# Attention on TensorE: written order, mixing in one piece, score banks spaced evenly

## The chip, the cores and the metric

The kernel runs on one core of a Trainium2 chip. The metric is the device time of one execution in microseconds (us). The core has five engines with an instruction stream each: TensorE (PE, with its weight loads as PEld), VectorE (DVE), ScalarE (ACT), GpSimd (POOL) and SyncE (SP), which here issues most of the DMAs. An engine works through its own stream in order and waits at semaphores for the others. All data is 32-bit floating point.

## The reference

The input x has 8 sequences of 512 tokens with 256 features. Four layers follow each other, each applied to the layer norm of x and added to x: a scan layer, a mixture of experts, causal attention, and the same mixture of experts again (same weights). Cut to what matters here:

```python
def _L0_attn_b_ref(x, Wqkv, Wout):
    B, T, D, H = (1, 1024, 256, 16)
    DK = D // H
    SCALE = 1.0 / float(np.sqrt(DK))
    ...
    scores = jnp.einsum('bhtd,bhsd->bhts', q, k) * SCALE
    scores = jnp.clip(scores, -10.0, 10.0)
    mask = jnp.triu(jnp.full((t, t), NEG, dtype=scores.dtype), k=1)
    scores = scores + mask[None, None, :, :]
    attn = jax.nn.softmax(scores, axis=-1)
    out = jnp.einsum('bhts,bhsd->bhtd', attn, v)
    out = out.transpose(0, 2, 1, 3).reshape(b, t, d)
    return jnp.einsum('btd,ed->bte', out, Wout)
...
x = x + _L0_attn_a_ref(_layernorm(x, axis=-1), ...)
x = x + _L0_ffn_ref(_layernorm(x, axis=-1), ...)
x = x + _L0_attn_b_ref(_layernorm(x, axis=-1), L0_attn_b_Wqkv, L0_attn_b_Wout)
x = x + _L0_ffn_ref(_layernorm(x, axis=-1), ...)
return x
```

Attention has 16 heads of 16 features, and t is 512. The mixture of experts has two shared experts, which see every token, and 16 routed ones, of which each token takes four, chosen by a router.

## The kernel before, in words

The kernel has four stages. A scan stretch runs the scan layer over the eight sequences and, in between, the shared experts and the routing of the sequences that are through. A routed stage then works off the routed experts of all tokens in blocks of 128 rows. An attention stretch does the same for attention and the second mixture, and a second routed stage ends the kernel. The change touches the attention stretch, about 810 to 1374 us of the profile.

**Attention of one sequence** (`main` of class `Attention`, line 998). Keys lie with the features of a head on 32 partitions, so that four heads stand in the four quarters of the array's rows. The 16 heads make four groups of four, (o, w). The weights of a group are made in three score steps (`weights`, line 1003): step 0 holds the first block of 128 keys against 512 queries, step 1 the fourth and the second block (128 and 384 queries), step 2 the third (256). What lies above the causal diagonal isn't computed. A step's matmuls (L1020, tile `ps_a`) use a quarter of the rows each and run side by side; they fill two PSUM tiles of kind `pair`, two banks each, of which there are two in all. ScalarE takes the exponentials (L1031, two per step, into `es_a` or a free part of `w_all`), and VectorE clips and masks (L1034, L1042).

**Mixing** (`mix`, line 1047) multiplies the weights with the values. Its matmuls (L1055, tile `po_a`) write 32 columns of the array each, again four side by side, and add up over the key blocks in one PSUM bank of kind `one`, of which there are four. A column of ones among the values gives the softmax's sum. `share` (line 1065) copies the sums on ScalarE (L1068), turns them with four TensorE transposes (L1071, tile `pto_a`) and divides on VectorE (L1073, L1074). After the four groups the output is turned (`turned`, line 353) and projected (`add_projection`, line 408).

**Order around the change.** Work is written as Python generators that yield a number of columns, their estimated TensorE work. `beside` (line 310) draws the next step from the piece that is least advanced by its share, and `timed` (line 326) places steps at given fractions of the whole. Beside attention of sequence b run: the projection to q, k, v of sequence b+1 (tiles `pq_a`, `pv_a`), the shared experts of sequence b-2 (`pg_m`, `pd_m`), routing of b-1 (transposes `pt_m`, router scores `pl_m`, counts `pr_m`), the norm and transposes of b+2 (`pt_l`) and scatters on POOL. Sequences 0 and 1 have no shared experts beside them, and sequence 7 has no projection. In the steps of attention, a score step of a group alternates with a mixing step of the group before:

```python
for i in range(len(BANKS)):
    yield weights(o, w, i, at)
    if last is not None:
        yield mix(*last[0:2], i, last[2])
if last is not None:
    share(*last)
```

This written order is where the scheduler of the tile framework starts, which then orders each engine's stream by when it takes the inputs to be ready. So in the compiled program neighbouring instructions of a step can be pulled apart. Buffers and semaphores follow from its order.

Of the kernel before, what the change touches and what calls it, by code (L numbers as in the profile page):

```python
# [15 lines left out]
P = 128  # L16
# [54 lines left out]
def tile_hybrid_block(  # L71
# [224 lines left out]

    class Piece:
# [48 lines left out]
    def issue(piece):  # L348
        for _ in piece.steps:
            pass  # L350


    def turned(src, tag: str, into, copies, home=None):

        rows = src()
        if home is None:
            dst = work.tile([P, KD, T], FP, tag="kb4", name=f"xT_{tag}", bufs=KB)
        else:
            dst = home(f"xT_{tag}")
        into(dst)  # L360
        for k in range(KD):
            pt = bank([P, NT, P], f"pt_{tag}_{k}")
            for t in range(NT):
                nc.tensor.transpose(pt[:, t, :], rows[:, t, k * P : (k + 1) * P], ident)
            flat = pt.rearrange("p t q -> p (t q)")
            copies[k](dst[:, k, :], flat)
            yield T // 2
# [40 lines left out]
    def add_projection(b: int, lhs_of, w_sb, n: int, tag: str):  # L408

        x_sb = x_tiles[b]  # L410
        for half in range(2):
            py = bank([P, 2, D], f"py_{tag}_{half}")
            for j in range(2):
                t = 2 * half + j
                for c in range(n):
                    nc.tensor.matmul(
                        py[:, j, :],
                        lhsT=lhs_of(c)[:, t * P : (t + 1) * P],
                        rhs=w_sb[:, c, :],
                        start=(c == 0),  # L420
                        stop=(c == n - 1),
                    )
                yield n * D
            rows = x_sb[:, 2 * half : 2 * half + 2, :]
            nc.vector.tensor_add(rows, py, rows)


    class Scan:
# [21 lines left out]
        def main(self, b: int, xnT):  # L450
            tag = f"s{b}"

            def steps():
                y_sb = []
                for c in range(NI):
                    pz = bank([P, T], f"pz_{tag}_{c}")
                    for k in range(KD):
                        nc.tensor.matmul(
                            pz,
                            lhsT=w_in_sb[:, k, c * P : (c + 1) * P],  # L460
                            rhs=xnT[:, k, :],
                            start=(k == 0),
                            stop=(k == KD - 1),
                        )
                    bias = b_in_sb[:, c : c + 1]
# [69 lines left out]
    def logits(i: int, b: int, tag: str, held):  # L535
        xnT = held["xnT"]
        pl = bank([P, NT, E], f"pl_{tag}")
        for t in range(NT):
            for k in range(KD):
                nc.tensor.matmul(  # L540
                    pl[:, t, :],
                    lhsT=xnT[:, k, t * P : (t + 1) * P],
                    rhs=rw_sb[:, k, :],
                    start=(k == 0),
                    stop=(k == KD - 1),
                )
            yield
# [4 lines left out]
    def choices(i: int, b: int, tag: str, held):  # L552
# [52 lines left out]
        flat = sel.rearrange("p t e -> p (t e)")  # L605
        nc.tensor.matmul(pr[:, 0].rearrange("p t e -> p (t e)"), lhsT=tri, rhs=flat, start=True, stop=True)
        nc.tensor.matmul(pr[:, 1].rearrange("p t e -> p (t e)"), lhsT=ones, rhs=flat, start=True, stop=True)
        row = small.tile([P, NT + 1, E], FP, tag="row", name=f"row_{tag}", bufs=3)
# [52 lines left out]
    def blocks(i: int, table):  # L661
# [60 lines left out]
        for c in range(CAND):  # L722
            nc.tensor.matmul(
                pe, lhsT=cand_e.to_broadcast([P, P]), rhs=chosen[:, c, :], start=(c == 0), stop=(c == CAND - 1)
            )
        expert = small.tile([P, NBLK], FP, tag="expert", name=f"expert_{tag}", bufs=1)
        nc.scalar.copy(expert, pe)
        lines = work.tile([1, 2, NBLK], I32, tag="col", name=f"lines_{tag}", bufs=COLS)
        for which in range(2):
            pl = bank([1, NBLK], f"pl_{tag}_{which}")  # L730
            for c in range(CAND):
                nc.tensor.matmul(
                    pl, lhsT=cand_at[:, which, c : c + 1], rhs=chosen[:, c, :], start=(c == 0), stop=(c == CAND - 1)
                )
            if which == 0:
# [11 lines left out]
    def routed(i: int, table, beside):  # L747
# [32 lines left out]
        def turn(n: int):  # L780
            rows = held[n][2]
            pt = bank([P, KD, P], f"pt_{i}_{n}", "misc")
            for k in range(KD):
                nc.tensor.transpose(pt[:, k, :], rows[:, k * P : (k + 1) * P], ident)  # L784
            nc.scalar.copy(rows[:, ROW : ROW + D], pt.rearrange("p k q -> p (k q)"))  # L785

        def up(n: int):
            w, _, rows = held[n]
            ph = bank([P, 2, F], f"ph_{i}_{n}", "big")
            for k in range(KD):  # L790
                nc.tensor.matmul(  # L791
                    ph.rearrange("p s f -> p (s f)"),
# [3 lines left out]
                    stop=(k == KD - 1),  # L796
                )
            act = rows[:, ROW + D : ROW + D + F]
# [16 lines left out]
        def turn_act(n: int):  # L815
            act = held[n][3]
            pt = bank([P, KF, P], f"pa_{i}_{n}", "misc")
            for f in range(KF):
                nc.tensor.transpose(pt[:, f, :], act[:, f * P : (f + 1) * P], ident)  # L819
            both = work.tile([P, 2, F], FP, tag="col", name=f"both_{i}_{n}", bufs=COLS)  # L820
# [3 lines left out]
        def down(n: int):  # L824
            w, _, rows, _, gain, both = held.pop(n)
            py = bank([P, D], f"pyr_{i}_{n}", "y")
            for f in range(KF):
                nc.tensor.matmul(  # L828
                    py,
# [3 lines left out]
                    stop=(f == KF - 1),  # L833
                )
            nc.scalar.mul(both[:, 1, :], py, gain[:, TK : TK + 1])  # L835
# [35 lines left out]
    def shared_experts(i: int, b: int, xnT_of, tanh: bool):  # L871
# [3 lines left out]
        def steps():  # L875
            xnT = xnT_of()
            acts = []
            for n in range(NSH):
# [3 lines left out]
                for f in range(KF):  # L882
                    pair = [bank([P, T], f"pg_{tag}_{n}_{f}_{which}") for which in range(2)]
                    for dst, w in zip(pair, (g_sb, u_sb)):
                        for k in range(KD):
                            nc.tensor.matmul(  # L886
                                dst,
# [3 lines left out]
                                stop=(k == KD - 1),  # L891
                            )
                        if dst is pair[0]:
# [14 lines left out]
            for half in range(2):  # L908
                py = bank([P, 2, D], f"pd_{tag}_{half}")
                for j in range(2):  # L910
                    t = 2 * half + j
                    for n in range(NSH):
                        for f in range(KF):
                            nc.tensor.matmul(  # L914
                                py[:, j, :],
# [3 lines left out]
                                stop=(n == NSH - 1 and f == KF - 1),  # L919
                            )  # L920
                    yield NSH * KF * D
# [17 lines left out]
    class Attention:  # L939
# [10 lines left out]
        def project(self, b: int, xnT):  # L950
# [8 lines left out]
            def steps():  # L959
                nc.gpsimd.memset(v_sb, 1.0)  # L960
                for o in range(NO):
                    for which in range(2):
                        pq = bank([P, T], f"pq_{tag}_{o}_{which}")
                        for k in range(KD):
                            nc.tensor.matmul(
                                pq,
# [3 lines left out]
                                stop=(k == KD - 1),  # L970
                            )
                        if which == 0:
# [5 lines left out]
                for h in range(2):  # L978
                    pv = bank([P, 2, D], f"pv_{tag}_{h}")
                    for j in range(2):  # L980
                        t = 2 * h + j
                        for k in range(KD):
                            nc.tensor.matmul(
                                pv[:, j, :],
# [3 lines left out]
                                stop=(k == KD - 1),  # L988
                            )
                        nc.scalar.copy(  # L990
# [7 lines left out]
        def main(self, b: int, made):  # L998
# [4 lines left out]
            def weights(o: int, w: int, i: int, at):  # L1003
# [12 lines left out]
                for c in tiles:  # L1016
                    n = T - c * P
                    for j in range(HG):
                        r = slice(32 * j, 32 * j + 32)
                        nc.tensor.matmul(  # L1020
                            ps[j // 2][:, j % 2, col : col + n],
# [3 lines left out]
                            stop=True,  # L1025
                        )
                        at[c, j] = es[j // 2][:, j % 2, col : col + n]
                    col += n
                mixed = len(tiles) * P
                for two in range(2):  # L1030
# [11 lines left out]
                    nc.vector.tensor_scalar(es[two][:, :, mixed:], es[two][:, :, mixed:], LOW, TOP, ALU.max, ALU.min)  # L1042
                return T + (len(tiles) - 1) * T

            order = [c for tiles, _ in BANKS for c in tiles]

            def mix(o: int, w: int, i: int, at):
# [4 lines left out]
                for c in BANKS[i][0]:  # L1052
                    for j in range(HG):
                        h = 8 * o + 2 * j + w
                        nc.tensor.matmul(  # L1055
                            at["po"][32 * j : 32 * j + 32, c * P : T],
# [4 lines left out]
                            tile_position=(0, 32 * j),  # L1061
                        )
                return len(BANKS[i][0]) * T

            def share(o: int, w: int, at):
# [4 lines left out]
                for t in range(NT):  # L1070
                    nc.tensor.transpose(pt[:, t].rearrange("p j c -> p (j c)"), oT[:, t * P : (t + 1) * P], ident)  # L1071
                rec = small.tile([P, NT, HG], FP, tag="rec", name=f"rec_{tag}_{o}_{w}")
# [267 lines left out]
```

## Time and profile before

| | us |
|---|---|
| median of 3 runs | 1834.43 |
| lowest, highest | 1831.78, 1835.23 |
| profiled execution | 1839.45 |
| its span, first to last instruction | 1837.7 |
| TensorE busy in the span | 1724.1 |
| first score step | 810.26 |
| last output projection of attention, next shared expert | 1315.99 |
| first transpose of the second routed stage | 1374.35 |

The profile page is of one execution. Busy time of an engine counts its instructions; for TensorE their ends are modelled, so that two starts say more than a length. A 32-bit matmul is recorded as two passes, a transpose as one, and `x8` behind a row counts records. `32*128` and `128*32` are the rows and columns of the array that a matmul uses. An arrow with an engine and a line names what ended an idle time.

### The profile page before, as it was taken

The page shows a single profiled execution, that of the slowest core. Times are in us where ns is not written, and L with a number is a line of the kernel's source. Part 1 is how long each engine was busy: PE and PEld are TensorE (multiplying, and loading weights), DVE is VectorE, ACT ScalarE, POOL GpSimd, SP SyncE. Part 2 cuts the span into 40 slices and gives each one's busy share as a digit, 9 for nine tenths or more (in the row PEclk, how much of TensorE's full clock was granted, in tenths as well). Part 3 has the DMA queues.
Part 4 walks back from the last instruction along what each step waited for, and adds up shares of the span by engine and source line. Part 5 has one row for each costly group of instructions (what it writes and reads, how often), then busy time and mean ns, then how long its engine had stood idle before and what let it go on. Part 6 is the DMA issues. An engine that isn't in the chain of part 4 may idle for free. (4 is left out here: it accounts for less than half of the span.)

```text
span 1837.7 us, 26953 instructions
## 1 busy us (share of the span) xinstructions
PE 1724.1 (94%) x7920; PEld 1026.4 (56%) x7920; DVE 1044.0 (57%) x3354; ACT 667.2 (36%) x1356; POOL 767.6 (42%) x667
## 2 busy tenths in 40 slices
PE   5899999899998999989999999999979999999992
PEld 3566666556665666644545545544545666566651
DVE  5878777444444444455776576666644444444442
ACT  2322222133333333345554454454313333333330
POOL 3255555435555555430042232232434555455542
PEclk9899999999999999999999999999989999999996
DMA  4444423345555555531011111121534555555557
GB/s 153 155 150 139 141 90 125 128 96 90 91 92 100 89 89 90 95 69 36 24 54 63 67 58 65 52 82 68 180 130 86 90 89 90 111 91 93 89 98 237
DMA packets 149968, 180.97 MB, mean 98 GB/s; under 512 B 16096, under 2 KB 136960, under 8 KB 149824
## 3 DMA queue, kind: packets, MB, share of 16 engines
q0 software_dynamic: 53136, 76.81, 22.6%
q1 hardware_dynamic: 94320, 96.12, 17.6%
q10 hardware_dynamic: 2368, 6.29, 0.9%
q8 instruction: 70, 1.15, 0.3%
q14 instruction: 74, 0.61, 0.1%
HBM read 81.62 MB, written 97.53 MB: 97 GB/s over the span
## 5 line engine op out<-in xcount | busy, mean ns | idle before, releaser
L836 POOL DMA_INDIRECT part<-both,rows x272 | 424.5, 1561 | 417.0 <-ACT both L835 384.8
L791 PE MATMUL ph<-w_all,rows 128*128 x1088 | 519.1, 600 | 1.2 <-ACT rows L785 0.6
L647 POOL DMA_INDIRECT xg<-sorted_m,slots_m x256 | 260.2, 1016 | 225.4 <-DVE sorted_m L637 110.3
L791 PEld LDWEIGHTS ph<-w_all,rows 128*128 128x128 f32 x1088 | 209.8, 193 | 152.1 <-issue 135.5
L800 DVE TENSOR_TENSOR rows<-ph,rows 128x256 f32<-128x256 f32 x272 | 115.2, 423 | 309.6 <-ACT rows L799 309.6
L828 PE MATMUL pyr<-w_all,both 128*128 x1088 | 283.1, 383 | 0.6 <-DVE both L821 0.6
L799 ACT ACTIVATE rows<-ph 128x256 f32<-128x256 f32 x272 | 104.2, 383 | 335.4 <-PE ph L791 335.4
L835 ACT ACTIVATE both<-pyr,gain 128x256 f32<-128x256 f32 x272 | 128.8, 473 | 215.1 <-ACT rows L785 176.3
L828 PEld LDWEIGHTS pyr<-w_all,both 128*128 128x128 f32 x1088 | 187.2, 192 | 15.3 <-ACT both L835 0.8
L784 PEld LDWEIGHTS pt<-ident,rows 128*128 128x128 f32 x544 | 76.6, 142 | 164.7 <-issue 152.7
L1031 ACT ACTIVATE w_all<-ps_a 128x1024 f32<-128x1024 f32 x128 | 124.3, 1021 | 82.2 <-PE ps_a L1020 73.9
L804 DVE SCALAR_TENSOR_TENSOR gain<-rows,expert_b 128x4 f32<-128x4 f32 x272 | 60.4, 222 | 129.5 <-ACT both L835 93.5
L1020 PE MATMUL ps_a<-w_all 32*128 32x512 f32 (+3 forms) x1024 | 119.6, 468 | 7.4 <-ACT w_all L1031 5.8
L886 PE MATMUL pg_m<-xT_m,su_sb 128*128 128x512 f32 x256 | 125.9, 614 | 0.0
L886 PE MATMUL pg_m<-xT_m,sg_sb 128*128 128x512 f32 x256 | 125.0, 611 | 0.0
L784 PE MATMUL pt<-ident,rows 128*128 128x128 f32 x544 | 105.0, 275 | 21.4 <-DMA rows<-xg 21.3
L819 PE MATMUL pa<-ident,rows 128*128 128x128 f32 x544 | 104.7, 274 | 17.5 <-DVE rows L801 9.4
L914 PE MATMUL pd_m<-sd_sb,act_m 128*128 128x256 f32 x512 | 121.1, 382 | 0.0
L821 DVE COPY both<-pa 128x256 f32<-128x256 f32 x272 | 112.6, 414 | 5.0 <-PE pa L819 5.0
L801 DVE TENSOR_TENSOR rows<-ph,rows 128x256 f32<-128x256 f32 x272 | 112.5, 414 | 0.1
L785 ACT COPY rows<-pt 128x256 f32<-128x256 f32 x272 | 99.9, 367 | 22.1 <-PE pt L784 22.1
L914 PEld LDWEIGHTS pd_m<-sd_sb,act_m 128*128 128x128 f32 x512 | 95.5, 190 | 21.1 <-issue 3.7
(199 smaller groups left out, 2071.0 us busy)
## 6 DMA issues: line engine op xcount, KB each, us to landing
rows<-xg SPq DMA_DIRECT2D x272, 136.0 KB, 2.6
part<-x SPq DMA_DIRECT2D x16, 512.0 KB, 2.8
part<-ys_m SPq DMA_DIRECT2D x16, 512.0 KB, 2.8
w_all<-in_L_ffn_gate_w_dram SPq DMA_DIRECT2D x24, 256.0 KB, 5.2
w_all<-in_L_ffn_up_w_dram SPq DMA_DIRECT2D x24, 256.0 KB, 5.5
w_all<-in_L_ffn_down_w_dram SPq DMA_DIRECT2D x24, 256.0 KB, 5.7
xg<-zeros SPq DMA_DIRECT2D x34, 136.0 KB, 1.8
part<-both,rows POOLq DMA_INDIRECT x272, 4.1
```

Of the source, the lines that this page charges most:

```text
L647: nc.gpsimd.indirect_dma_start(out=xg[i], out_offset=bass.IndirectOffsetOnAxis(ap=slots[:, at : at + 1], axis=0), in_=rows[:, t, :], in_of ...
L784: nc.tensor.transpose(pt[:, k, :], rows[:, k * P : (k + 1) * P], ident)
L791: nc.tensor.matmul(ph.rearrange("p s f -> p (s f)"), lhsT=rows[:, ROW + k * P : ROW + (k + 1) * P], rhs=w_all[:, bass.ds(w + k * 2 * F, 2 ...
L800: nc.vector.tensor_mul(act, ph[:, 0, :], act)
L821: nc.vector.tensor_copy(both[:, 0, :], pt.rearrange("p k q -> p (k q)"))
L828: nc.tensor.matmul(py, lhsT=both[:, 0, f * P : (f + 1) * P], rhs=w_all[:, bass.ds(w + 2 * KD * F + f * D, D)], start=(f == 0), stop=(f == ...
L835: nc.scalar.mul(both[:, 1, :], py, gain[:, TK : TK + 1])
L836: nc.gpsimd.indirect_dma_start(out=parts[i][n % 2], out_offset=bass.IndirectOffsetOnAxis(ap=rows[:, D + 2 * TK : D + 2 * TK + 1].bitcast(U ...
L886: nc.tensor.matmul(dst, lhsT=w[:, k, f * P : (f + 1) * P], rhs=xnT[:, k, :], start=(k == 0), stop=(k == KD - 1),)
L914: nc.tensor.matmul(py[:, j, :], lhsT=acts[n][:, f, t * P : (t + 1) * P], rhs=shared[n][3][:, f, :], start=(n == 0 and f == 0), stop=(n == ...
L1020: nc.tensor.matmul(ps[j // 2][:, j % 2, col : col + n], lhsT=k_sb[w][r, o, c * P : (c + 1) * P], rhs=q_sb[r, o, c * P : T], start=True, st ...
L1031: nc.scalar.activation(es[two], ps[two][:, :, 0:cols], AF.Exp, scale=ATT_SCALE)
```

## The change

A helper `ordered` pins a TensorE instruction behind the one traced before it, by an ordering that waits for nothing. It wraps every matmul and transpose of the kernel, and acts only while the list `strict` is not empty, that is, around the attention stretch with its tail of shared experts. There the compiled order of TensorE is the written one.

The order of `steps` is new: score step 0 of a group, then all three mixing steps of the group before in one go, then `share` of that group, then score steps 1 and 2. The yielded columns are new as well (9, 2, 12 and 9 times 128 per group), which sets how much other work is drawn in between. The transposes of the output are issued in one go. Computation, tiles and buffers are the same.

```diff
+    strict = []
+
+    def ordered(made):
+        if strict:
+            tc.keep_in_program_order(made)
...
-                        nc.tensor.matmul(
+                        ordered(nc.tensor.matmul(
                             ps[j // 2][:, j % 2, col : col + n],
...
-                return T + (len(tiles) - 1) * T
...
-                        nc.tensor.matmul(
+                        ordered(nc.tensor.matmul(
                             at["po"][32 * j : 32 * j + 32, c * P : T],
...
-                return len(BANKS[i][0]) * T
...
+                def mixed(o: int, w: int, at):
+                    for i in range(len(BANKS)):
+                        mix(o, w, i, at)
+
                 last = None
-                for o, w, at in groups:
-                    for i in range(len(BANKS)):
-                        yield weights(o, w, i, at)
-                        if last is not None:
-                            yield mix(*last[0:2], i, last[2])
+                for group in groups:
+                    weights(*group[0:2], 0, group[2])
+                    if last is not None:
+                        mixed(*last)
+                    yield 9 * P
                     if last is not None:
                         share(*last)
-                        yield T // 2
-                    last = o, w, at
-                for i in range(len(BANKS)):
-                    yield mix(*last[0:2], i, last[2])
+                    yield 2 * P
+                    weights(*group[0:2], 1, group[2])
+                    yield 12 * P
+                    weights(*group[0:2], 2, group[2])
+                    yield 9 * P
+                    last = group
+                mixed(*last)
+                yield 9 * P
                 share(*last)
-                yield T // 2
-                yield from turned(lambda: held["o"], f"o{tag}", lambda oT: held.update(oT=oT), by_both)
+                yield 10 * P
+                issue(Piece(0, turned(lambda: held["o"], f"o{tag}", lambda oT: held.update(oT=oT), by_both)))
+                yield 9 * P
                 yield from add_projection(b, lambda c: held["oT"][:, c, :], wo_sb, KD, tag)
 
-            each = 2 * NT * T + T // 2
-            return Piece(2 * NO * each + KD * T // 2 + NT * KD * D, steps())
+            return Piece((2 * NO * 32 + 28) * P + NT * KD * D, steps())
...
+    strict.append(True)
     with banks_of(one=4, pair=2):
         table = stretch(Attention())
+    strict.clear()
```

More of the change, by code (lines that the diff above doesn't have):

```diff
@@ L363, in turned @@
             for t in range(NT):
-                nc.tensor.transpose(pt[:, t, :], rows[:, t, k * P : (k + 1) * P], ident)
+                ordered(nc.tensor.transpose(pt[:, t, :], rows[:, t, k * P : (k + 1) * P], ident))
             flat = pt.rearrange("p t q -> p (t q)")
@@ L421, in add_projection @@
                         stop=(c == n - 1),
-                    )
+                    ))
                 yield n * D
@@ L463, in steps @@
                             stop=(k == KD - 1),
-                        )
+                        ))
                     bias = b_in_sb[:, c : c + 1]
@@ L539, in logits @@
             for k in range(KD):
-                nc.tensor.matmul(
+                ordered(nc.tensor.matmul(
                     pl[:, t, :],
@@ L545, in logits @@
                     stop=(k == KD - 1),
-                )
+                ))
             yield
@@ L605, in choices @@
         flat = sel.rearrange("p t e -> p (t e)")
-        nc.tensor.matmul(pr[:, 0].rearrange("p t e -> p (t e)"), lhsT=tri, rhs=flat, start=True, stop=True)
-        nc.tensor.matmul(pr[:, 1].rearrange("p t e -> p (t e)"), lhsT=ones, rhs=flat, start=True, stop=True)
+        ordered(nc.tensor.matmul(pr[:, 0].rearrange("p t e -> p (t e)"), lhsT=tri, rhs=flat, start=True, stop=True))
+        ordered(nc.tensor.matmul(pr[:, 1].rearrange("p t e -> p (t e)"), lhsT=ones, rhs=flat, start=True, stop=True))
         row = small.tile([P, NT + 1, E], FP, tag="row", name=f"row_{tag}", bufs=3)
@@ L722, in blocks @@
         for c in range(CAND):
-            nc.tensor.matmul(
+            ordered(nc.tensor.matmul(
                 pe, lhsT=cand_e.to_broadcast([P, P]), rhs=chosen[:, c, :], start=(c == 0), stop=(c == CAND - 1)
-            )
+            ))
         expert = small.tile([P, NBLK], FP, tag="expert", name=f"expert_{tag}", bufs=1)
@@ L731, in blocks @@
             for c in range(CAND):
-                nc.tensor.matmul(
+                ordered(nc.tensor.matmul(
                     pl, lhsT=cand_at[:, which, c : c + 1], rhs=chosen[:, c, :], start=(c == 0), stop=(c == CAND - 1)
-                )
+                ))
             if which == 0:
@@ L783, in turn @@
             for k in range(KD):
-                nc.tensor.transpose(pt[:, k, :], rows[:, k * P : (k + 1) * P], ident)
+                ordered(nc.tensor.transpose(pt[:, k, :], rows[:, k * P : (k + 1) * P], ident))
             nc.scalar.copy(rows[:, ROW : ROW + D], pt.rearrange("p k q -> p (k q)"))
@@ L790, in up @@
             for k in range(KD):
-                nc.tensor.matmul(
+                ordered(nc.tensor.matmul(
                     ph.rearrange("p s f -> p (s f)"),
@@ L796, in up @@
                     stop=(k == KD - 1),
-                )
+                ))
             act = rows[:, ROW + D : ROW + D + F]
@@ L818, in turn_act @@
             for f in range(KF):
-                nc.tensor.transpose(pt[:, f, :], act[:, f * P : (f + 1) * P], ident)
+                ordered(nc.tensor.transpose(pt[:, f, :], act[:, f * P : (f + 1) * P], ident))
             both = work.tile([P, 2, F], FP, tag="col", name=f"both_{i}_{n}", bufs=COLS)
@@ L827, in down @@
             for f in range(KF):
-                nc.tensor.matmul(
+                ordered(nc.tensor.matmul(
                     py,
@@ L833, in down @@
                     stop=(f == KF - 1),
-                )
+                ))
             nc.scalar.mul(both[:, 1, :], py, gain[:, TK : TK + 1])
@@ L885, in steps @@
                         for k in range(KD):
-                            nc.tensor.matmul(
+                            ordered(nc.tensor.matmul(
                                 dst,
@@ L891, in steps @@
                                 stop=(k == KD - 1),
-                            )
+                            ))
                         if dst is pair[0]:
@@ L913, in steps @@
                         for f in range(KF):
-                            nc.tensor.matmul(
+                            ordered(nc.tensor.matmul(
                                 py[:, j, :],
@@ L919, in steps @@
                                 stop=(n == NSH - 1 and f == KF - 1),
-                            )
+                            ))
                     yield NSH * KF * D
@@ L964, in steps @@
                         for k in range(KD):
-                            nc.tensor.matmul(
+                            ordered(nc.tensor.matmul(
                                 pq,
@@ L970, in steps @@
                                 stop=(k == KD - 1),
-                            )
+                            ))
                         if which == 0:
@@ L982, in steps @@
                         for k in range(KD):
-                            nc.tensor.matmul(
+                            ordered(nc.tensor.matmul(
                                 pv[:, j, :],
@@ L988, in steps @@
                                 stop=(k == KD - 1),
-                            )
+                            ))
                         nc.scalar.copy(
@@ L1019, in weights @@
                         r = slice(32 * j, 32 * j + 32)
-                        nc.tensor.matmul(
+                        ordered(nc.tensor.matmul(
                             ps[j // 2][:, j % 2, col : col + n],
@@ L1025, in weights @@
                             stop=True,
-                        )
+                        ))
                         at[c, j] = es[j // 2][:, j % 2, col : col + n]
@@ L1054, in mix @@
                         h = 8 * o + 2 * j + w
-                        nc.tensor.matmul(
+                        ordered(nc.tensor.matmul(
                             at["po"][32 * j : 32 * j + 32, c * P : T],
@@ L1061, in mix @@
                             tile_position=(0, 32 * j),
-                        )
-                return len(BANKS[i][0]) * T
+                        ))
             def share(o: int, w: int, at):
@@ L1070, in share @@
                 for t in range(NT):
-                    nc.tensor.transpose(pt[:, t].rearrange("p j c -> p (j c)"), oT[:, t * P : (t + 1) * P], ident)
+                    ordered(nc.tensor.transpose(pt[:, t].rearrange("p j c -> p (j c)"), oT[:, t * P : (t + 1) * P], ident))
                 rec = small.tile([P, NT, HG], FP, tag="rec", name=f"rec_{tag}_{o}_{w}")
```

## The prediction

> **What bounds the kernel now.** I began with the page's first two parts. TensorE is busy nearly all the time:
>
> ```profile
> PE 1724.1 (94%) x7920; PEld 1026.4 (56%) x7920; DVE 1044.0 (57%) x3354; ACT 667.2 (36%) x1356; POOL 767.6 (42%) x667
> ```
>
> The change touches only the attention stretch, so next I cut the span into windows, one per sequence, at the starts of the first score matmuls (810.3, 859.5, 910.0, 979.7 us and so on). Columns: window, length, busy us and instructions of PE, PEld, DVE, ACT, POOL, then clock and DMA.
>
> ```profile
> 810.00:859.50 49.50, 46.28 (x342) 21.17 (x340) 31.00 (x78) 28.67 (x40) 2.77 (x4) 1.00 0.05 18
> 859.50:910.00 50.50, 48.66 (x365) 23.82 (x364) 37.66 (x122) 30.28 (x42) 3.11 (x3) 1.00 0.10 32
> 979.70:1048.90 69.20, 69.06 (x429) 35.31 (x428) 46.20 (x144) 33.76 (x48) 19.83 (x20) 1.00 0.18 63
> 1256.10:1316.00 59.90, 58.22 (x392) 29.56 (x392) 43.17 (x142) 29.27 (x39) 24.08 (x25) 1.00 0.42 139
> ```
>
> Sequences 2 to 6 take 68 to 70 us with TensorE never idle and ScalarE half idle: TensorE's order is the bound there. Sequences 0 and 1 have little work to put between the heads, and TensorE is idle for 3.2 and 1.8 us. The list of waits over the whole stretch shows for what:
>
> ```profile
> PE ps_a L1020 <- ACT w_all L1031: 5.8, 12, 1.0
> PE ps_a L1020 <- ACT es_a L1031: 0.9, 3, 0.4
> ```
>
> A busy TensorE isn't an efficient one, so third I read the timeline of one group of four heads (sequence 3). Columns: start, length, engine, line, what, records merged.
>
> ```profile
> 1002.48 1.14 PE L1020 MATMUL ps_a<-w_all 32*128 32x512 f32 x8
> 1003.55 1.98 PE L886 MATMUL pg_m<-xT_m,sg_sb 128*128 128x512 f32 x4
> 1005.46 1.06 PE L1055 MATMUL po_a<-w_all,v_a 128*32 128x512 f32 x8
> 1006.46 1.15 PE L1020 MATMUL ps_a<-w_all 32*128 32x128 f32 x16
> 1007.54 1.98 PE L886 MATMUL pg_m<-xT_m,su_sb 128*128 128x512 f32 x4
> 1009.36 0.60 PE L364 MATMUL pt_m<-ident,sorted_m 128*128 128x128 f32 x4
> 1009.89 1.07 PE L1055 MATMUL po_a<-w_all,v_a 128*32 128x128 f32 x16
> ...
> 1013.24 0.71 PE L1020 MATMUL ps_a<-w_all 32*128 32x256 f32 x8
> 1013.88 0.64 PE L1055 MATMUL po_a<-es_a,v_a 128*32 128x256 f32 x8
> 1014.45 1.98 PE L886 MATMUL pg_m<-xT_m,su_sb 128*128 128x512 f32 x4
> ```
>
> Starts count here, not lengths. Back to back, four passes of 512 columns (pg) take 1.72 us, or 0.43 each: at 1319.42, 1321.14 and 1322.86 three follow each other. A score step (ps, 32 rows) runs its four heads side by side, two passes of 512, so it should take 0.86; it takes 1.07. Start to start minus streaming, over all pairs of the stretch without an idle gap, gives a price for each change of shape: leaving row-tiled scores +0.21, leaving column-tiled mixing (po) +0.14, full matmul into either +0.20, full matmul into transpose +0.10, transpose into either +0.10, transpose into full +0.05, full into full 0.01.
>
> The second loss is a step that is cut in two. Four heads share the array only if they stand together; here one head's scores stand alone between two transposes:
>
> ```profile
> 1040.36 1.12 PE L1020 MATMUL ps_a<-w_all 32*128 32x512 f32 x2
> 1041.42 0.66 PE L364 MATMUL pt_oa<-ident,o_a 128*128 128x128 f32 x4
> ...
> 1048.91 1.13 PE L1020 MATMUL ps_a<-w_all 32*128 32x512 f32 x6
> ```
>
> One head costs 1.06 us, three heads again 1.06.
>
> [...] two exponentials of 1.02 us follow each 1.07 us of scores, and in sequences 0 and 1 that is what TensorE waits for. All other prices are durations of this trace.
>
> **The change, part by part.** The changed program's TensorE list can be read without running it. Outside the stretch it is as before; SP's and POOL's lists are in the same order too (but for a swap among reloads of gate and up weights behind attention), so no DMA moves past another. In a steady sequence the list now reads: scores 0, all mixing of the group before, filler, transposes of the mixed heads, scores 1, filler, scores 2, filler.
>
> *Changes of shape*, counted in a steady sequence (before, after): leaving scores 14, 12, saves 2 x 0.21 = 0.42; leaving mixing 12, 4, saves 8 x 0.14 = 1.12; full into tiled 15, 11, saves 0.80; transpose into tiled 7, 2, saves 0.50; full into transpose 6, 5, saves 0.10; transpose into full 1, 5, and router scores (pl) into full 1, 2, cost 0.23. Sum 2.7 us.
>
> *Cut steps*: the lone head (0.86 streaming) and a 256-column step cut by v's projection (0.43): 1.3 us. In sequences 2 to 6 together 4.0 us each, so 5 x 4.0 = 20 us.
>
> *Waits that the fixed order adds there.* Behind a waiting TensorE instruction everything waits. Scores 1 to scores 2: the second exponential ends 0.11 + 2.04 after scores 1, the filler is 2.3 us or more in three groups and 1.91 in the last, so 0.3 us are lost. Transposes behind mixing: the copy L1068 needs 0.11 + 0.60 + 0.05; a filler of 1.06 or more stands there, without it 0.8 would show. Mixing needs the last clips on VectorE, about 1.5 us behind the exponential; scores 0 and the first 1.7 us of mixing cover them. VectorE has 46 us of work for 65. The old waits (69.2 against 68.4 from streaming and prices) are 0.8 and I leave them for the new ones. Score buffers and the four single banks get easier: po is held some 3 us instead of a whole group.
>
> *Sequences 0 and 1.* Streaming and prices fall from 43.1 to 38.5 and from 46.3 to 41.5, but ScalarE's pace shows (already now: 49.2 less 43.1 is 6.1 of waiting, of which the trace books 3.2 as idle because ends of matmuls are modelled). Walking sequence 0's list with the durations above: scores 2 right behind scores 1 in two groups, 2.2 lost each; transposes right behind mixing in three, 0.8 each; scores 0 right behind scores 2 once, 1.2; scores 1 at the start 0.4; scores 2 of the last two groups 0.3 and 1.1; the end of the last mixing 0.3; output projection behind its copies 0.9. That is 11.0, so 49.5 against 49.2 now. Sequence 1 the same way: 41.5 + 9.8 = 51.3 against 50.5. Together +1.1.
>
> *Sequence 7 with its tail* (1256.1 to 1353.5, 97.3 us): streaming and prices 90.5, waits 0.35 + 0.8 + 0.3 + 1.2 + 0.45 + 0.7 = 3.8, so 94.3: saves 3.0. What follows (scatters, then the first routed rows, 10.6 us of idle TensorE at 1363.8) hangs on the last route and moves along.
>
> Sum: -20 + 1.1 - 3.0 = -21.9. The profiled execution took 1839.45 with a span of 1837.7; the median of the runs is 5.0 lower and I take the saving from it: 1834.4 - 21.9 = about 1812.5.
>
> **Rivals.** (1) *The early sequences gain too*: if the waits of 0 and 1 come out about as large as now, they and sequence 7 give 4.6 to 4.8 each: -20 - 14 = -34, 1800. For it: the exponentials' total, 24 us of 49, isn't a limit by itself. Against: groups with nothing between scores 1 and 2. (2) *Half eaten*: 0.5 us of new waits per group in sequences 2 to 6 (a late filler input, a bank, VectorE working off norms of 0.4 us apiece), 20 x 0.5 = 10: 1822. Nothing in the trace reorders TensorE around such a wait any more. (3) *Slower*: the wait of the gapless groups, scores 2 behind the exponentials of scores 1, in all groups. At 2.2 us in 20 more groups it is +44, so 1834.4 - 22 + 44 = 1856; it decides from 1.1 us per group on (22 / 20). Against: ScalarE is busy 33.8 of 69.2 us, and 1.9 us of filler stands between. (4) *No effect*: the old order re-established by other waits; the list says otherwise, so it could only come as a balance near zero.
>
> **How the numbers follow.** Main case 0.57, own range 1806 to 1819; (1) 0.13; (2) 0.15; (3) 0.10; (4) 0.05. A measurement here tells about 0.2%, 3.7 us, from no change. Main, (1) and nearly all of (2) are faster: 0.84; same 0.06; slower 0.10. The range takes in (1) and (2): 1800 to 1829.
>
> **What would show it.** Windows from first scores to first scores should shrink from 69.2 to about 65 in sequences 2 to 6 and stay near 50 in 0 and 1. Mixing should appear as one piece of 32 records with 2.29 us to the next start; no score step of 2 or 6 records should be left. Waits of ps for L1031 should rise, mostly before 910 us, from 6.7 to 12 or more. I am wrong if steady windows stay above 68, if TensorE idles there for VectorE or for filler inputs, or if time before 800 or after 1375 us changes.

## The result, and the profile after

The change made the kernel slower. The median of six runs is 1843.6 us (1842.06 to 1850.28), against 1834.1 for the kernel before, measured beside it: a ratio of 1.0054, interval 1.004 to 1.0068. The forecast was 1812.5, with a range of 1800 to 1829, so both the sign and the range were wrong.

The page of the changed kernel shows TensorE less busy than before, by 20.8 us:

```profile
PE 1703.3 (93%) x7920; PEld 1025.1 (56%) x7920; DVE 1047.3 (57%) x3354; ACT 667.2 (36%) x1356; POOL 767.9 (42%) x667
```

The work became cheaper, and time was still lost. Windows of the changed kernel, cut at first score steps: sequences 0, 1, 3, and the start of 7, in the columns of the prediction's windows.

```profile
807.90:860.70 52.80, 46.43 (x337) 22.95 (x336) 31.19 (x80) 28.85 (x40) 2.77 (x4) 0.94 0.03 8
860.70:916.00 55.30, 48.99 (x365) 24.65 (x364) 39.11 (x122) 30.55 (x42) 3.11 (x3) 0.97 0.09 29
985.70:1055.50 69.80, 66.36 (x429) 35.12 (x428) 46.31 (x144) 33.76 (x48) 20.00 (x20) 1.00 0.18 63
1260.70:1320.00 59.30, 55.75 (x391) 30.04 (x391) 42.47 (x139) 29.38 (x39) 24.16 (x25) 0.97 0.46 152
```

Sequence 3 had 69.06 us of TensorE work in 69.20; it now has 66.36 in 69.80. All of the saving, and a little more, is idle time. In sequences 0, 1 and 7 the granted clock, 1.00 before, is below one. The list of TensorE's waits over the stretch, changed kernel:

```profile
PE ps_a L1027 <- ACT w_all L1038: 11.3, 22, 1.4
PE po_a L1061 <- DVE es_a L1049: 5.6, 9, 0.7
PE pv_a L990 <- ACT v_a L997: 4.4, 7, 0.7
PE po_a L1061 <- DVE w_all L1041: 4.1, 6, 0.8
PE pto_a L1076 <- ACT oT_a L1073: 3.5, 5, 0.7
PE ps_a L1027 <- ACT es_a L1038: 2.5, 2, 2.0
```

Mixing (`po_a`) waits for VectorE, 9.7 us in all; the list of before has no such row. Lengths of the sequences in us, first score step to first score step (the last with its tail). In the kernel before, one head's scores of sequences 3 to 7 stood 8.5 us ahead of the other three, and the three count as the start:

| sequence | 0 | 1 | 2 | 3 | 4 | 5 | 6 | 7 and tail |
|---|---|---|---|---|---|---|---|---|
| before | 49.2 | 50.5 | 69.7 | 69.2 | 69.2 | 70.0 | 68.1 | 97.3 |
| predicted | 49.5 | 51.3 | 65.7 | 65.2 | 65.2 | 66.0 | 64.1 | 94.3 |
| after | 52.9 | 55.2 | 69.7 | 69.8 | 69.8 | 70.0 | 65.5 | 97.2 |

From the first score step to the first transpose of the second routed stage it is 564.1 us before and 571.0 after, +6.9. The rest of the span differs from execution to execution by as much (1266.5 to 1274.3 us over the twelve undisturbed profiles of this study), so the medians decide on the whole and the lengths above on where. The medians are 9.5 us apart; the 2.6 us beyond the 6.9 are within this spread and are not placed.

**Where sequences 2 to 5 lose it.** Timeline of TensorE in the changed kernel: the mixing of the first group of sequence 3, then that of the second group.

```profile
996.41 1.14 PE L1027 MATMUL ps_a<-w_all 32*128 32x512 f32 x8
997.48 1.43 PE L1061 MATMUL po_a<-w_all,v_a 128*32 128x512 f32 x12
999.65 1.18 PE L1061 MATMUL po_a<-w_all,v_a 128*32 128x128 f32 x12 [0.74 <-DVE w_all L1041]
1001.50 0.63 PE L1061 MATMUL po_a<-es_a,v_a 128*32 128x256 f32 x4 [0.67 <-DVE es_a L1049]
1002.71 0.63 PE L1061 MATMUL po_a<-es_a,v_a 128*32 128x256 f32 x4 [0.58 <-DVE es_a L1049]
1003.26 1.13 PE L990 MATMUL pv_a<-w_att,xT_l 128*128 128x256 f32 x4
...
1013.22 1.93 PE L1061 MATMUL po_a<-w_all,v_a 128*32 128x512 f32 x24
1014.96 0.61 PE L1061 MATMUL po_a<-es_a,v_a 128*32 128x256 f32 x8
1015.51 1.98 PE L893 MATMUL pg_m<-xT_m,su_sb 128*128 128x512 f32 x4
```

The second mixing is what was predicted: one piece of 32 records, 1013.22 to 1015.51, 2.29 us. The first takes 5.78, that is 3.49 more. Only 1.99 of this stand in brackets; the rest is packing that is lost when a wait falls between heads which would have run side by side (pieces of 12 and 4 records in place of 24 and 8). VectorE's own timeline of the changed kernel says why the clips are late:

```profile
990.72 0.41 DVE L407 TENSOR_SCALAR sorted_m<-x,mv_m,rstd_m 128x256 f32<-128x256 f32 x1
991.04 0.42 DVE L1041 SCALAR_TENSOR_TENSOR w_all<-w_all,causal 128x256 f32<-128x256 f32 x1
991.38 0.55 DVE L1049 TENSOR_SCALAR w_all<-w_all 128x768 f32<-128x768 f32 x1
994.91 1.23 DVE L141 TENSOR_TENSOR x<-x,more 128x1024 f32<-128x1024 f32 x1 [2.98 <-issue]
...
998.93 0.67 DVE L1041 SCALAR_TENSOR_TENSOR w_all<-w_all,causal 128x512 f32<-128x512 f32 x1
...
1002.37 0.28 DVE L1049 TENSOR_SCALAR es_a<-es_a 128x256 f32<-128x256 f32 x1
```

L141 adds the two parts of the residual stream of sequence b+2. VectorE stands 2.98 us in front of it, and the clips of score steps 1 and 2 of the first group lie behind it, up to 1002.65. Its row says `issue`, that is, the profile names nothing that ended the wait; but the load of x landed at 994.83, 0.08 us before the sum starts, and the trace of before names this load. SP could issue it only when the norm at 990.72 had read an older sequence out of the buffer, for which its queue waited 1.8 us:

```profile
991.16 0.36 SPq L139 DMA_DIRECT2D x<-part  x1
```

The same stand was in the trace of before, where it cost nothing:

```profile
988.96 1.22 DVE L141 TENSOR_TENSOR x<-x,more 128x1024 f32<-128x1024 f32 x1 [3.27 <-DMA x<-part]
```

There mixing went in three steps, at 990.73, 994.72 and 1000.16 in that sequence. Each needed only its own step's clips, and those were through by then.

### The profile page after: what moved, and what is told of

It reads as the page before. It is cut to its first block, busy times and chain, and to the rows that moved or that the text cites. A ratio compares the mean times of both kernels' runs of the same rounds, so it can differ in the third digit from the quotient of the medians.

```text
span 1840.3 us, 26966 instructions
## 1 busy us (share of the span) xinstructions
PE 1703.3 (93%) x7920; PEld 1025.1 (56%) x7920; DVE 1047.3 (57%) x3354; ACT 667.2 (36%) x1356; POOL 767.9 (42%) x667
## 5 line engine op out<-in xcount | busy, mean ns | idle before, releaser
L1038 ACT ACTIVATE w_all<-ps_a 128x1024 f32<-128x1024 f32 x128 | 124.1, 1021 | 70.9 <-PE ps_a L1027 69.2
L1027 PE MATMUL ps_a<-w_all 32*128 32x512 f32 (+3 forms) x1024 | 107.8, 472 | 14.1 <-ACT w_all L1038 11.3
```

Of the source, the lines that this page charges most:

```text
L1038: nc.scalar.activation(es[two], ps[two][:, :, 0:cols], AF.Exp, scale=ATT_SCALE)
```

## The experiments

Whole times are medians in us; each ratio is to the kernel before, measured beside it on the same chip. The expectations name the theories by letters. P: pinning costs the time; M: mixing in one piece costs it; E: the loss in sequences 0 and 1 is separate, and goes when these two have their old order; V: VectorE's stand at the sum delays the first mixing; D: VectorE is late there by its own work, and the sum only stands in idle time.

**1. The new order without pinning.**

```diff
-    strict.append(True)
```

> The new order of steps and the new columns, without pinning TensorE. Theory P (the pinning is what costs: behind a waiting instruction nothing can be drawn forward): sequences 0 and 1 fall back to 49 to 51 us from 52.9 and 55.2, and the kernel takes 1834 to 1836 us. Rival M (mixing in one piece costs, because it asks for all weights of a group at once): sequence 3 still stands behind VectorE for 1 to 2 us at its first mixing, sequences 0 and 1 stay above 52, and the kernel takes 1840 to 1846.

1837.76, ratio 1.0013 (1.0003 to 1.0023): between the two expectations. Lengths 48.7, 54.6, then 70.0, 70.1, 70.1, 70.4, 65.8 and 94.5. So pinning costs in sequences 0 and 7. The steady sequences are as long without it, and mixing waits for VectorE as much (6.5 and 4.5 us in the list of waits, against 5.6 and 4.1).

**2. The old order with pinning.** The diff is the one above turned round: `steps` and the yields of the kernel before, `strict` left on.

> The old order of steps and columns, with TensorE pinned. Theory P: 1840 us or more, with sequences 0 and 1 above 52 us. Rival M: the score steps cut in two are whole again (about 2.2 us less streaming and changes of shape in each of sequences 2 to 6, 3.5 in 0 and 1), nothing asks for all weights at once, and the kernel is faster than before: 1822 to 1832.

1846.0, ratio 1.007 (1.0047 to 1.0092), as P has it. Sequences 0 and 1 take 54.3 and 55.4, 2 to 5 take 69.3 to 70.2, and the list of waits has none of mixing for VectorE. Rival M had some 2 us less in each steady sequence, from score steps that are whole again; its list of waits has others instead, which were not followed up (over the whole stretch 6.2 us of `pto_a` for ScalarE, 4.1 of `pq_a` for VectorE). Each half of the change is bad in a place of its own.

**3. Sequences 0 and 1 in the old order and unpinned, the rest as changed.**

```diff
+            if b < 2:
+                return Piece(..., old_steps())
...
+            if i == 1 and b == 2:
+                strict.append(True)
```

> The changed kernel, but sequences 0 and 1 keep the old order of steps and are not pinned; from sequence 2 on all as changed. Theory E (these two, with little work between the heads, cost 3.7 and 4.7 us of the whole): 8 us faster than the changed kernel, about 1835, level with before; sequences 0 and 1 at 49 to 51. Rival: the loss moves into sequence 2, and it stays above 1840.

1833.81, ratio 0.9999 (0.9988 to 1.001). Sequences 0 and 1 are back at 49.2 and 50.0, the steady ones stay at 69.8 to 70.1: the loss in the first two is separate, and accounts for all by which the change is slower. The expected gain of the others is still missing.

**4. The sum moved, too far.** The sum is issued at the start of the norm that needs it, a third into the sequence.

```diff
         x_tiles[b] = x_sb
-        nc.vector.tensor_add(x_sb, x_sb, more)
+        unsummed[b] = more
...
         x_sb = x_tiles[b]
+        if b in unsummed:
+            tc.keep_in_program_order(nc.vector.tensor_add(x_sb, x_sb, unsummed.pop(b)))
```

> The changed kernel, but the sum of the two loaded parts of a sequence (VectorE, 1.22 us, which stood idle 3 us ahead of it for the load while clips of the first group lay behind it) is pinned to the start of the norm that needs it, a third into the sequence. Theory V (the first mixing of sequences 2 to 5 loses 3.5 us because VectorE's queue stands at this sum): those sequences fall from 69.8 to about 66.3, sequence 1 by up to 2.3, and the kernel is 14 to 17 us faster than the changed one, 1827 to 1830. Rival D (VectorE is simply late with clips and routing there, with or without the sum): at most 1.2 us a sequence, 1838 or more.

1870.75, ratio 1.0194 (1.0177 to 1.0211). The waits of the first mixing went, down to one of 0.6 us, but V's number failed by 40 us. The list of waits, VectorE's and TensorE's rows:

```profile
DVE xn L414 <- POOL rstd_l L411: 39.0, 5, 9.6
```

```profile
PE pl_m L554 <- DVE o_a L1086: 18.8, 4, 4.9
PE pl_m L554 <- DVE xT_m L378: 10.2, 4, 2.6
```

The norm behind the sum takes a power on GpSimd (`rstd`), which now came after the 16 scatters of a sequence (1.0 us each and 0.3 between). VectorE stood for it 9.6 us at most, in order again, and TensorE's router scores behind VectorE. Sequence 1 fell from 55.2 to 52.9, as V had it; sequences 2 to 5 rose to 75.8 to 77.2. For these the run settles nothing on V; it shows the same fault in another place.

**5. The sum at 0.14 of the sequence, and three companions.** The place is behind the clips of the first group and ahead of most scatters. Beside it: the same with experiment 3; the kernel before with the sum moved likewise; and the changed kernel with a fourth buffer for x, so that the load comes earlier and the sum stays (for room, eight in place of nine buffers of 4 KB).

```diff
+                def summed(b=nxt):
+                    tc.keep_in_program_order(nc.vector.tensor_add(x_tiles[b], x_tiles[b], unsummed.pop(b)))
+                    yield
+                pieces.append(timed(summed(), 0.14))
```

> The changed kernel with one VectorE instruction moved: the sum of the two loaded parts of sequence b+2 is no longer issued with its loads, but pinned at 0.14 of the sequence, behind the clips of the first group. Theory V (VectorE stands some 3 us in order at this sum, waiting for its DMA, and the clips of the first group lie behind it; the mixing in one piece waits for them): the waits of po for VectorE go, sequences 2 to 5 fall from 69.8 to 66 to 67 us each, and the whole from 1843.6 to 1828 to 1832. Theory D (VectorE is late there by its own work, the sum only stands in the idle time before it): sequences 2 to 5 lose 1.2 us or less each, 1839 to 1844. A late norm or scatter, as when the sum went a third in, would show as waits of VectorE for GpSimd and sequences above 72.

> Both repairs together: sequences 0 and 1 in the old order and unpinned, the others as in the changed kernel, and the sum moved to 0.14 of the sequence. If the two losses are separate, they add: sequences 0 and 1 at 49 and 50, sequences 2 to 5 at 66 to 67, so 1833.8 less 12 to 15, that is 1819 to 1823, below the kernel before by 0.6 to 0.8%. If theory D holds, 1829 to 1834, the same as before.

> Control: the kernel before with the sum moved in the same way. Its mixing goes step by step and asks for the clips later, so theory V expects no more than 1 us per sequence, 1830 to 1836. If the sum's wait costs every order alike, it falls by 3 us per sequence too, to 1818 to 1824.

> The changed kernel with the load itself earlier: four buffers of x in place of three, so that the loads of sequence b+2 don't wait for the rows of an older sequence to be sorted (and eight in place of nine buffers of 4 KB, for room). The sum stays where it was. Theory V expects the waits of po for VectorE to go here too, sequences 2 to 5 at 66 to 67 and 1828 to 1834; theory D 1839 or more. If the lost 4 KB buffer matters, waits for DMAs or shared experts' tiles appear instead.

The four came out at 1915.0, 1907.7, 1930.0 and 1950.7, the kernel before itself at 1951.9: on that chip every kernel was held up at times, with TensorE, ScalarE and VectorE standing together for up to 10 us, so nothing is read from these times. All were run again, the changed kernel with them.

> The same kernel as mid_sum (the changed kernel, the sum of the loaded parts at 0.14 of the sequence), once more, since all kernels of that call, the one before too (1951.9), were held up for 5 to 10 us at a time at points where TensorE, ScalarE and VectorE stood together. Undisturbed, its trace so far says: the waits of the first mixing are gone, the one behind v's copies (1.0 us) and the one at the last group (1.5) stay, so 66.3 per sequence in 2 to 5, 52.9 in 0 and 1, and 1827 to 1832, a ratio of 0.996 to 0.999. Theory D: 1839 to 1844, 1.003 to 1.005.

> The same kernel as x4 (the load earlier by a fourth buffer of x, eight in place of nine 4 KB buffers), once more. Theory V: the waits of po for VectorE are gone, 66 to 67 in sequences 2 to 5, 1828 to 1834. Theory D: 1839 or more. If the 4 KB buffer matters, something else waits.

> The same kernel as early_mid (sequences 0 and 1 in the old order and unpinned, and the sum at 0.14), once more. If the two losses are separate, 49.2, 50.0, then 66.3 in sequences 2 to 5, 65.5 and 97: 1818 to 1823, a ratio of 0.991 to 0.994. Theory D: 1829 to 1834.

> The changed kernel itself beside its variants on one chip, so that they can be compared with it and not only with the kernel before: a ratio of 1.004 to 1.007, sequences 2 to 5 at 69.8.

| kernel | median | ratio | 95% interval | sequences 0, 1 | 2 to 5 | 7 and tail |
|---|---|---|---|---|---|---|
| changed (after2) | 1843.49 | 1.0045 | 1.003 to 1.0059 | 51.6, 55.2 | 69.7 to 69.8 | 97.3 |
| its sum at 0.14 (mid_sum2) | 1824.77 | 0.9949 | 0.9931 to 0.9967 | 52.8, 52.8 | 66.3 | 97.2 |
| its load earlier (x4_2) | 1828.0 | 0.9963 | 0.9953 to 0.9972 | 52.7, 52.8 | 66.3 | 97.2 |
| with 0 and 1 as before (early_mid2) | 1820.94 | 0.9934 | 0.9908 to 0.996 | 49.2, 50.0 | 66.3 to 66.5 | 97.3 |

V holds: two unlike edits, one that takes the sum out of the way and one that lets its data come sooner, bring the steady sequences to the same 66.3, each 3.5 us shorter. Sequence 1, where VectorE stood 3.19 us at the same sum (870.05), loses 2.4 with either. For the whole, V had 1827 to 1832 and 1828 to 1834; the first came out 2 us below, the second at the edge. D, which had 1839 or more, fails in both. Why their medians differ by 3.2 us with equal stretches (554.5 us) was not looked into; their intervals overlap. Timeline of TensorE with the sum at 0.14, first mixing of sequence 3, then VectorE's sum, which no longer waits:

```profile
995.40 1.93 PE L1066 MATMUL po_a<-w_all,v_a 128*32 128x512 f32 x24
997.15 0.61 PE L1066 MATMUL po_a<-es_a,v_a 128*32 128x256 f32 x8
997.69 1.13 PE L995 MATMUL pv_a<-w_att,xT_l 128*128 128x256 f32 x4
```

```profile
994.78 0.28 DVE L1054 TENSOR_SCALAR es_a<-es_a 128x256 f32<-128x256 f32 x1
...
995.71 1.22 DVE L1241 TENSOR_TENSOR x<-x,more 128x1024 f32<-128x1024 f32 x1
```

The first mixing is 2.29 us too, and with the earlier load as well (993.82 to 996.11). In this kernel's list of waits those for VectorE have shrunk from 9.7 us to

```profile
PE po_a L1066 <- DVE es_a L1054: 0.6, 1, 0.6
```

The two losses add, as expected of early_mid2, but for the 2.4 us of sequence 1, which both edits take away. Its stretch is 548.3 us, against 571.0 of the changed kernel and 564.1 before.

**6. The control, and the order unpinned with its sum moved.**

> The kernel before with the sum of the loaded parts moved to 0.14 of the sequence. If only mixing in one piece asks for the clips of the first group too early, 1832 to 1836, ratio 0.998 to 1.001, and sequences 2 to 5 stay at 69 to 70. If the wait at the sum costs the old order alike, 3 us per sequence are gained, 1820 to 1824.

> The new order without pinning (order_only, 1837.8), with the sum at 0.14 of the sequence. If the sum's wait is what its first mixing loses, sequences 2 to 5 fall from 70.1 to 66.5 to 67.5, and the whole to 1823 to 1828, ratio 0.993 to 0.996; sequence 0 stays near 49. If the scheduler's shuffles are what costs there, 1834 to 1838.

The kernel before with its sum moved: 1833.97, ratio 0.9992 (0.9982 to 1.0003), sequences 2 to 5 at 68.9 to 69.0. The old order has next to nothing from it; only mixing in one piece asks for the clips early enough. The new order unpinned with its sum moved: 1817.35, ratio 0.9916 (0.9894 to 0.9939), below its expected band by 6 us, and the lowest time of all kernels here. Lengths 48.7, 51.4, four times 66.6, 65.8, 94.5. The sum's place was what the unpinned order lost, not the scheduler's shuffles. All of it in one table, ratios to the kernel before:

| order of attention | sum with its load | sum at 0.14 |
|---|---|---|
| old, unpinned | 1 | 0.9992 |
| new, unpinned | 1.0013 | 0.9916 |
| new and pinned, but 0 and 1 old and unpinned | 0.9999 | 0.9934 |
| new, pinned (the change) | 1.0045 | 0.9949 |

**What pinning does in sequences 0, 1 and 7.** Part is the waits that the prediction walked. Another part is the clock. Two neighbouring windows of the changed kernel, sequence 0, and TensorE's timeline in the second of them:

```profile
807.90:814.40 6.50, 4.66 (x29) 1.79 (x28) 5.13 (x15) 5.13 (x7) 1.24 (x2) 1.00 0.17 61
814.40:821.80 7.40, 7.38 (x20) 2.65 (x20) 4.04 (x10) 2.76 (x4) 0.32 (x1) 0.54 0.00 0
```

```profile
814.42 2.14 PE L1027 MATMUL ps_a<-w_all 32*128 32x256 f32 x8 [0.91 <-ACT w_all L1038]
816.49 3.78 PE L972 MATMUL pq_a<-xT_l,w_att 128*128 128x512 f32 x4
820.20 1.68 PE L1027 MATMUL ps_a<-w_all 32*128 32x512 f32 x8
```

After 6.5 us with 1.84 idle the granted clock is 0.54 for 7.4 us. What this costs can be read from a second execution of the same kernel (after2), in which the clock was full at this place:

```profile
819.28 0.70 PE L1027 MATMUL ps_a<-w_all 32*128 32x256 f32 x4 [0.91 <-ACT w_all L1038]
820.20 0.70 PE L1027 MATMUL ps_a<-w_all 32*128 32x256 f32 x4 [0.21 <-ACT w_all L1038]
820.83 1.98 PE L972 MATMUL pq_a<-xT_l,w_att 128*128 128x512 f32 x4
822.74 1.14 PE L1027 MATMUL ps_a<-w_all 32*128 32x512 f32 x8
```

The same three steps, from the start of the first to the mixing behind them, take 4.53 us there (819.28 to 823.81) and 7.38 at the lower clock (814.42 to 821.80). So the clock costs 2.85 us in sequence 0. In after2 the clock is halved later in that sequence (from 832.12 on) and costs 1.6, and its sequence 0 is 1.2 us shorter: the same kernel, and a different length by where the clock falls. The same reckoning gives 1.7 in sequence 1 (mixing at 902.74 takes 3.98 us in place of 2.29) and 1.6 in sequence 7 (5.47 from 1294.41 to 1299.88; at full clock 1.55, as in after2 from 1297.90 on, and 2.29), 6.2 in all. In the unpinned new order (with the sum moved) sequence 0 keeps full clock:

```profile
807.50:856.20 48.70, 44.08 (x337) 21.90 (x336) 30.18 (x79) 28.77 (x40) 2.42 (x4) 1.00 0.03 12
```

In the profiles of the kernel before and of the changed one the clock changes only at the edges of a grid of steps of 3.41 us: the stretches at half clock last 3.41, 6.83, 10.24 or 13.65 us, but for the last of each profile (34.97 and 34.60). Windows of the changed kernel, cut at such edges, before and during its three halvings, and three steps that no halving followed, the last of them ahead of the stretch:

```profile
811.09:814.50 3.41, 1.71 (x18) 0.90 (x18) 3.38 (x13) 2.86 (x5) 1.34 (x2) 1.00 0.00 0
814.50:821.33 6.83, 6.83 (x20) 2.57 (x20) 3.50 (x10) 2.66 (x4) 0.22 (x1) 0.50 0.00 0
899.84:903.25 3.41, 1.84 (x16) 0.81 (x20) 2.07 (x5) 3.37 (x6) 0.00 (x0) 1.00 0.02 5
903.25:906.66 3.41, 3.41 (x32) 1.16 (x24) 3.17 (x21) 0.21 (x1) 0.00 (x0) 0.50 0.00 0
1292.37:1295.78 3.41, 1.39 (x11) 0.60 (x8) 2.08 (x11) 3.06 (x5) 2.80 (x3) 1.00 0.59 199
1295.78:1299.19 3.41, 3.41 (x26) 1.19 (x28) 3.27 (x20) 1.74 (x2) 0.23 (x2) 0.50 0.11 41
872.53:875.94 3.41, 2.10 (x20) 0.59 (x20) 3.41 (x15) 0.73 (x2) 0.00 (x0) 1.00 0.00 0
1138.77:1142.18 3.41, 1.80 (x16) 0.45 (x16) 3.41 (x16) 0.36 (x1) 1.12 (x1) 1.00 0.01 2
776.95:780.37 3.42, 1.49 (x5) 0.48 (x4) 0.55 (x1) 0.76 (x3) 1.18 (x1) 1.00 0.89 187
```

TensorE is idle for 50, 46 and 59% of the steps ahead of the halvings, and for 38, 47 and 56% of the last three. From the first scores to the last shared experts of the stretch the two profiles hold 314 such steps at full clock, 158 before and 156 after. Both with more than 48% of idle time are followed by half the clock, one of the eight with 35 to 47%, and none of the other 304. So in the stretch the halvings went with the idle share of a step and not with the length of one gap: in sequence 0 the longest gap of the step was 0.91 us, and no halving followed the step at 824.74 (38%), which holds a gap of 1.16 us (in front of 827.77). From what share on a halving comes is not shown: with 46% it came, with 47 and 56% it did not. The pinned order's waits bring such steps in sequences 0, 1 and 7. Unpinned, the granted clock is 1.00 in these sequences: in the kernel before (1.00 from 810.00 to 1353.50), in the new order (order_only), and, for sequences 0 and 1, in the new order with the sum moved (order_mid).

## Why the prediction was wrong

Point by point, against the profile's +6.9 where -21.9 was forecast, 28.8 apart:

- **Changes of shape, cut steps: right.** TensorE's busy time fell 20.8 us, no score step of 2 or 6 records is left (9 each before), and mixing is one piece of 32 records in 26 of 32 groups; waits cut the others. With the sum moved, a steady sequence takes 66.3, of the 65.2 to 66.0 forecast.
- **Waits of the steady sequences: the step that failed.** It was the sentence that mixing needs the last clips on VectorE, that scores 0 and the first 1.7 us of mixing cover them, and that VectorE has 46 us of work for 65. That is an average over a sequence. In VectorE's list the clips stood behind a sum, the sum behind a load, and the load behind a buffer, and in the trace no clip went past the sum: VectorE stood for 2.98 us up to 994.91, with every later clip behind it. What was taken for slack was partly this stand. It costs 3.5 us in each of four sequences, 14.1 together by experiment 5, half of the error, and 2.4 more in sequence 1. The line to look up was in the trace of before: the 3.27 us at 988.96. The prediction had listed "if TensorE idles there for VectorE" as what would prove it wrong.
- **The other waits of sequences 2 to 6, too small.** Scores 2 of the last group were put at 0.3 us. They lose 1.5, since a table load of 1.28 us stands ahead of the exponentials (ScalarE at 1034.68), and the table loads (the rows ACT_TABLE_LOAD of ScalarE) were not in the walk. The values' projection behind its own copies (`pv_a`, about 1.0 us) was not in it at all. What the allowance for old waits did not cover of this is 3.1 us in sequences 2 to 5 (262.1 forecast and 14.1 for the sum, of 279.3) and 1.4 in sequence 6: 4.5 of the error.
- **Sequences 0 and 1: waits nearly right, clock missed.** Streaming and prices of 38.5 leave 14.4 of sequence 0 for waits; less 2.9 for the clock that is 11.5, where the walk had 11.0. Sequence 1 has 13.7; less 1.7 for the clock and 2.4 for a mixing that waits for VectorE behind the same sum it is 9.6, where the walk had 9.8. The prediction took 1.00 for the clock without saying so, as the windows of before showed it.
- **Sequence 7: its wait too short, clock missed.** It is 2.9 us longer than forecast: 1.6 for the clock and 1.3 for a wait put at 1.2. This wait is 2.02 in brackets and 0.5 more for the second pair of heads (1.55 in place of 1.07), and two table loads of 1.28 around the router's sigmoid stood before the exponentials. Unpinned the sequence takes 94.5, of 94.3 forecast.
- **The rivals.** The slower one had the right side and the wrong mechanism: scores 2 behind the exponentials in all groups. In the steady sequences they wait in the last group only. VectorE being late was among the causes of "half eaten", at 0.5 us per group; it was 3.5 in one group of four.
- **Behind the tail** nothing moved, as forecast: from its end to the first transpose of the second routed stage it is 20.9 us in both.
- **A small reading.** Two exponentials were put at 2.04 us, twice 1.02; in the trace a pair takes 1.94, since the second starts before the first has ended. Nothing above hangs on it.

Added up: 14.1 and 2.4 for VectorE's stand at the sum, 4.5 for other waits of sequences 2 to 6, 6.2 for the clock, 1.3 for the wait of sequence 7 and 0.3 for the waits of sequences 0 and 1: 28.8.

## What to carry to other kernels

When a change makes one engine ask for several inputs sooner, don't ask whether the producer has time on average: read the producer's own list of instructions ahead of each input and look for one that waits for a transfer. Moving such an instruction a few us down cost nothing here where nobody was waiting, and it decided what the reordering was worth: neither edit gained alone (0.9992 and 1.0013), and both together gave 0.9916. Moved too far, it cost 27 us. And fix an order only where the engine has work to fill it: where it hadn't, in sequences 0, 1 and 7, the waits cost the clock besides, 6.2 us here.

## What was not expected of the hardware

- The waits between heads cost more than their length: 1.99 us of waits in a mixing of 2.29 us made it 5.78, because the four column tiles no longer ran side by side (the 256-column step as two pieces, at 1001.50 and 1002.71, in place of one at 1014.96).
- In sequence 0 the clock was halved after a step of 3.41 us of which TensorE was idle for half (1.71 us busy), in gaps of 0.91 us at most. The three halvings cost 6.2 us in all, and two executions of one kernel had the first of them at different places.
- A wait for a buffer reached TensorE through three queues: SP's load at 991.16, VectorE's sum at 994.91, mixing at 999.65.
